# k and v of the last two pairs through two levels of seven products, their chain on VectorE

## The chip, the cores and the metric

One core of one Trainium2 chip runs the whole program. The metric is the device time of one execution in microseconds (us). Engine names in the profile: PE is TensorE's matrix multiplies, PEld its weight loads, DVE is VectorE, ACT is ScalarE, POOL is GpSimd, SP issues the DMAs. All data is float32.

## The reference

The input `x` is 8 sequences of 512 tokens by 512 features. After a layernorm `xn`:

```python
q = xn @ Wq.T + bq;  k = xn @ Wk.T + bk;  v = xn @ Wv.T + bv
phi_q, phi_k = elu(q) + 1, elu(k) + 1
kv_sum = cumsum(phi_k * v, axis=1)                  # along the tokens
s = (phi_q * kv_sum) * 32 ** -0.5 @ Wo.T + bo
g = silu(ffn(xn))    # Hadamard transforms folded into weights; gate and up 512 -> 2048, down 2048 -> 512
out = x + s * g
```

## The kernel before, in words

**Pairs.** The sequences are worked on two at a time, so the loop over `p` has four pairs of 1024 tokens. For each pair: attention projections k, v, q; four hidden units of the feed-forward part (gate and up for 512 hidden features each); `project_out`; and `down` in two halves, after units 1 and 3. Features lie on the 128 partitions, tokens along the free dimension.

**Seven products in place of eight.** Every matrix product is cut into 2 x 2 blocks and done with seven block products (P1 to P7) and sums of blocks. The factors of the weights are made once and kept in DRAM; the factors of the tokens, `xo`, are made per pair by `inner_tokens` and `inner_t3`.

- One level: `group` (products on line 460) does k, v, q with 128x512 products. One call covers two of the four feature blocks of k, v or q, seven products of two matmuls each; k and v need four calls a pair.
- Two levels: `block_product` (products on line 638) does one of the seven outer products by seven inner ones, each two matmuls of 128x256. `hidden_unit` calls it seven times, in the order P1, P5, P6, P2, P7, P3, P4, with gate and up as the two lanes. This is how all hidden units but three of pair 0 are done.

**Reading PSUM.** In a `block_product` each of the seven inner products is followed by a read: `px` (three banks) is read after its products 1, 3, 4 and 5 of the chain into `sa`, `sb`, `sc` or straight to the output; `py` (one bank) and `pz` (two banks) are added to those. Where the outer product adds to an earlier result (`add` is given: P6, P2, P7, P3, P4), all seven reads are on DVE; else four are copies on ACT and three are on DVE (lines 646 to 680). A bank is free for the next product only after its read.

**Attention before.** `with_k` makes elu(k)+1 from two ACT activations and one DVE instruction per half (lines 710 to 712); `with_v` multiplies (724); `sums` runs the cumulative sum (729); `with_q` makes the context `co` (737), whose token factors POOL makes (`encode_tokens`, lines 304 to 307).

**Units.** In `hidden_unit` POOL adds tiles (lines 838 and 842), ACT applies Silu (828), POOL or, in units 1 and 3, DVE multiplies gate by up (829) and makes the token factors of `ho` (823).

**Order.** An agenda (`at`, `advance`) places the steps of a group by hand, so that the products of two neighbours interleave. `later` puts small steps into a list that `pace` takes from after an output has been issued; `catch_up` empties it. A scheduler then orders the instructions of each engine; every engine works through its own list in order. `queue` is the order in which weights are streamed in, three ahead, through four buffers; loads and stores are issued by SP in order. Working tiles of 8 KB a partition come from the pool `t8`, which has six buffers: a new tile waits until an old one has been read for the last time.

Of the kernel before, what the change touches and what calls it, by code (L numbers as in the profile page):

```python
# [21 lines left out]
def kernel(  # L22
# [81 lines left out]
    at = 0  # L104
# [12 lines left out]
    had = const.tile([P, P], F32, tag="had", name="had")  # L117
    ones = const.tile([P, 1], F32, tag="ones", name="ones")
    su_ug = const.tile([P, KD], F32, tag="su_ug", name="su_ug")
    su_dp = const.tile([P, NF], F32, tag="su_dp", name="su_dp")  # L120


# [207 lines left out]
    def stream_w(name):  # L330
        w = new_w("%s_%s" % (name[0], name[1] if type(name[1]) is int else "%d_%d" % name[1]))
        if name[0] == "gu":
            u, i = name[1]
            nc.sync.dma_start(w, inner[u][:, i])
        elif name[0] == "down":
            h, i = name[1]
            assert wd_made[h] == 4
            w = by_factor(w, 4)
            nc.sync.dma_start(w, wd[h][:, i])
        else:  # L340
            nc.sync.dma_start(flat(w), kept["%s_%d" % name])
            if name[0] == "o":
                w = by_factor(w)
        return w
# [77 lines left out]
        later(0.0, at, 8, last, soon=True)  # L422

    agenda = []
# [199 lines left out]
        between()  # L627


    def block_product(name, w, x, out, add, done):  # L630


        px, py, pz = (bank(t, name, 2) for t in ("px", "py", "pz"))
        sums = {}

        def product(p, i, first):
            for lane in range(2):
                nc.tensor.matmul(  # L638
                    p[:, lane], w[:, lane, i, :], x[:, i, :],
                    start=(first and lane == 0), stop=True, skip_group_check=True,  # L640
                )

        def read(what, m, q):
            s = snap.tile([P, 2, H], F32, tag="s", name=f"{what}_{name}")
            if add is None:
                nc.scalar.copy(s, px)
            else:
                nc.vector.tensor_tensor(s, px, add[:, m, :, q], ALU.add)  # L648
            return s

        def p1():
            product(px, P1, True)
            sums["a"] = read("sa", 0, 0)

        def p2():
            product(py, P2, True)
            nc.vector.tensor_tensor(out[:, 0, :, 0], sums["a"], py, ALU.add)

        def p7():
            product(pz, P7, True)  # L660

        def p6():
            product(px, P6, False)
            sums["b"] = read("sb", 1, 0)

        def p5():
            product(px, P5, False)
            sums["c"] = read("sc", 1, 1)
            nc.vector.tensor_tensor(out[:, 1, :, 1], sums["c"], pz, ALU.add)

        def p3():
            product(px, P3, False)
            if add is None:
                nc.scalar.copy(out[:, 0, :, 1], px)
            else:
                nc.vector.tensor_tensor(out[:, 0, :, 1], px, add[:, 0, :, 1], ALU.add)  # L676

        def p4():
            product(pz, P4, False)
            nc.vector.tensor_tensor(out[:, 1, :, 0], sums["b"], pz, ALU.add)  # L680
            if done:
                done()

        for place, fn in ((0, p1), (2, p2), (3, p7), (4, p6), (8, p5), (12, p3), (13, p4)):
            at(place, fn)
        advance(7)
# [2 lines left out]
    def x_rhs(xo):  # L689
        return lambda k, i: xo[:, i, k : k + 3 : 2, :]  # L690

    def attention(p, xo, co, get_w):
        def project(m, g, then):
            w = get_w(m, g)
            r = t8.tile([P, 2, 2, L], F32, tag="t", name=f"{m}_{p}_{g}")
            b = (col("b" + m, g), col("b" + m, g + 2))

            def whole(px):
                nc.scalar.activation(r[:, 0, 1], px, AF.Identity, bias=b[0])
                then(r)  # L700

            group(
                f"{m}_{p}_{g}", [w[:, 0], w[:, 1]], x_rhs(xo),
                (r[:, 0, 0], r[:, 1, 0], r[:, 1, 1]), whole, b, 1.7,
            )

        def elu_plus_one(r, name):
            neg = t8.tile([P, 2, 2, L], F32, tag="t", name=f"neg_{name}")
            for h in range(2):
                nc.scalar.activation(neg[:, h], r[:, h], AF.Relu, scale=-1.0)  # L710
                nc.scalar.activation(neg[:, h], neg[:, h], AF.Exp, scale=-1.0)
                nc.vector.scalar_tensor_tensor(r[:, h], r[:, h], 1.0, neg[:, h], ALU.add, ALU.max)

        def heads(g):
            phi = {}
# [23 lines left out]
                    )  # L739
                encode_tokens(nc.gpsimd, co[:, g])  # L740

            project("k", g, with_k)
            project("v", g, with_v)
            project("q", g, with_q)

        for g in range(2):
            heads(g)


    def put_by(name, t):  # L750
# [56 lines left out]
            (r[:, 0, 0], r[:, 1, 0], r[:, 1, 1]), with_up,  # L807
        )

    def hidden_unit(p, u, xo, ho, get_w, last):  # L810

        def new(name):
            return t8.tile([P, 2, 2, 2, H], F32, tag="t", name=f"{name}_{p}_{u}")

        def outer(i, out, add=None, done=None):
            w = get_w("gu", (u, i))
            block_product(f"gu_{p}_{u}_{i}", w, xo[:, i], out, add, done)

        def whole(t, lane):
            return t[:, :, lane].rearrange("p m q t -> p m (q t)")  # L820

        def sub(eng, c, a, b):
            eng.tensor_tensor(ho[:, :, c], ho[:, :, a], ho[:, :, b], ALU.subtract)

        def gated(t, a, s, eng):
            g = whole(t, 0)
            for m in range(2):
                nc.scalar.activation(g[:, m], g[:, m], AF.Silu, scale=col("w_gate", u + m * NU + a * NG))  # L828
            eng.tensor_tensor(ho[:, :, (P1, P7, P2, P3)[2 * a + s]], g, whole(t, 1), ALU.mult)

        eng = nc.vector if last else nc.gpsimd
        ra, rv, ru1 = new("a"), new("v"), new("u1")
        rest = {}

        def with_u1():
            rest["u3"] = r = new("u3")
            for m in range(2):
                nc.gpsimd.tensor_tensor(r[:, m], ru1[:, m], rv[:, m], ALU.add)  # L838

        def with_r():  # L840
            for m in range(2):
                nc.gpsimd.tensor_tensor(rv[:, m], rv[:, m], rr[:, m], ALU.add)  # L842
            gated(rv, 1, 1, nc.gpsimd)

        def with_c12():
            gated(rest["u3"], 0, 1, eng)
            sub(eng, P5, P7, P1)
            sub(eng, P6, P3, P5)
            sub(eng, P7, P3, P7)

        def with_c21():
            gated(ru1, 1, 0, eng)
            sub(eng, P4, P2, P6)

        outer(P1, ra)
        outer(P5, rv)
        outer(P6, ru1, ra, with_u1)
        outer(P2, ra, ra, lambda: gated(ra, 0, 0, nc.gpsimd))
        rr = new("r")
        outer(P7, rr, ru1, with_r)  # L860
        while "u3" not in rest:
            advance(1)
        outer(P3, rest["u3"], rest["u3"], with_c12)
        outer(P4, ru1, rr, with_c21)

    def down(p, half, hos, get_w, ds=None, ss=None, ys=None):
        if half == 0:
# [212 lines left out]

    queue = []
    for p in range(B // 2):
        queue += [(p, m, g) for g in range(2) for m in ("k", "v", "q")]
        for u in range(NU):
            if p == 0 and u < NU - 1:
                queue += [(p, m, f) for m in ("gate", "up") for f in (u, u + NU)]
            else:
                queue += [(p, "gu", (u, i)) for i in (P1, P5, P6, P2, P7, P3, P4)]
            if u == 0:
                at_o = len(queue) - (2 if p == 0 else 0)  # L1090
                queue[at_o:at_o] = [(p, "o", 0), (p, "o", 1)]
            if u % 2:
                queue += [(p, "down", (u // 2, i)) for i in (P1, P7, P2, P6, P5, P3, P4)]
# [56 lines left out]
    for b in range(2):  # L1150
        transposed(b, xs[b], xo)
    nc.vector.memset(ones, 1.0)
    nc.vector.tensor_scalar(su_ug, col("su_ug", 0, KD), D ** -0.5, None, ALU.mult)
    nc.vector.scalar_tensor_tensor(
        su_dp, col("su_dp", 0, NF), FF ** -0.5, col("w_up", 0, NF), ALU.mult, ALU.mult
    )
# [45 lines left out]
    for p in range(B // 2):  # L1202
        if p:
            catch_up()
            inner_tokens(xo)
            co = hop.tile([P, 2, 7, L], F32, tag="h", name=f"co_{p}")
        attention(p, xo, co, get_w)
        if p:
            catch_up()
            inner_t3(xo, (P1, P5, P6, P2, P7))  # L1210
            at(9, lambda: inner_t3(xo, (P3, P4)))
        more = p + 1 < B // 2
        hos = []
        for u in range(NU):
# [8 lines left out]
            else:  # L1223
# [4 lines left out]
                    with background():  # L1228
                        normalized(3)
                ho = hop.tile([P, 2, 7, L], F32, tag="h", name=f"ho_{p}_{u}")  # L1230
                hidden_unit(p, u, xo, ho, get_w, u % 2 == 1)
                if u == 0:
                    project_out(p, co, get_w)
            hos.append(ho)
            if more and u < 2 and (p, u) != (0, 1):
# [2 lines left out]
            if u == 1:  # L1238
                if p == 0:
                    weights_ahead(NU - 1)  # L1240
                    inner_tokens(xo, 6)
                down(p, 0, hos, get_w)
                hos = []
        ds = [fetch(f"d_{p}_{s}") for s in range(2)]
# [59 lines left out]
```

## Time and profile before

| what | value |
| --- | --- |
| median of 3 runs | 1551.32 us (1550.75 to 1551.83) |
| span of the profiled execution | 1552.4 us |
| granted TensorE clock, mean | 0.998 |
| PE busy | 1523.8 us, 98% |
| DVE busy | 1002.4 us, 65% |
| ACT busy | 418.9 us, 27% |
| POOL busy | 436.7 us, 28% |
| one pair (first k product of pair 1 to that of pair 2, by the chain of waits) | 460.67 to 823.82 us |

The page gives no time for the profiled execution other than its span, which lies 1.1 us above the median of the runs; times worked out on the trace are set against the span, and 1.1 us is taken off to compare with runs. A line of the timeline has the start in us, the time from the first start to the last end in us, the engine, the line, the operation, tiles, shapes and the number of records merged. TensorE leaves two records for each float32 matmul in the program. An instruction's own time has an end that overlaps with the next; the spacing of starts in an unbroken stream is what one more instruction costs.

### The profile page before, as it was taken

How to read it: one execution, taken by the hardware profiler on the slowest of the kernel's cores; microseconds unless marked ns; L12 is line 12 of the kernel's file. 1: busy time of each engine (PE TensorE's matmuls, PEld its weight loads, DVE VectorE, ACT ScalarE, POOL GpSimd, SP SyncE). 2: the span in 40 equal slices, each digit the busy share in tenths (PEclk: the TensorE clock that was granted, in tenths of full speed). 3: DMA queues.
4: the chain of work that ended last, by engine and by line, in shares of the span. 5: the costliest groups of instructions: out<-in, count | busy, mean ns of one | idle time of the engine just before them, and what ended most of it. 6: DMA issues, size and time to landing. Idle time of an engine off the chain costs nothing.

```text
span 1552.4 us, 15693 instructions
## 1 busy us (share of the span) xinstructions
PE 1523.8 (98%) x5924; PEld 1121.3 (72%) x5924; DVE 1002.4 (65%) x1423; ACT 418.9 (27%) x664; POOL 436.7 (28%) x236
## 2 busy tenths in 40 slices
PE   7989999999999999999999999999999999999998
PEld 3436446746874588888884488888886478888887
DVE  7989787378867665516767674715675575533673
ACT  4452341141125411112114431111213431111211
POOL 1232233004320261205511144302621126210631
PEclk9999999999999999999999999999999999999999
DMA  8345877687985244354576344335574233535462
GB/s 276 98 141 176 258 250 240 214 276 261 267 283 162 90 154 160 95 166 164 166 265 235 93 143 149 114 119 186 175 245 155 87 112 102 191 100 174 164 258 81
DMA packets 197692, 273.31 MB, mean 176 GB/s; under 512 B 56816, under 2 KB 155120, under 8 KB 193392
## 3 DMA queue, kind: packets, MB, share of 16 engines
q1 hardware_dynamic: 197472, 272.27, 54.0%
q8 instruction: 47, 0.77, 0.2%
q14 instruction: 29, 0.24, 0.0%
q10 hardware_dynamic: 144, 0.03, 0.0%
HBM read 196.25 MB, written 76.02 MB: 175 GB/s over the span
## 4 chain that ended last, share of the span: by engine, by line
PE 90%; DVE 6%; DMA 1%; ACT 1%; issue 1%; SPq 0%; POOL 0%; POOLq 0%; DVEq 0%; ACTq 0%
PE px_gu L638 20%; PE px_dn L536 13%; PE pz_gu L638 10%; PE pz_dn L536 6%; PE py_gu L638 5%; PE px_k L460 4%; PE py_dn L536 4%; PE px_o L536 3%; PE px_v L460 3%; PE px_q L460 3%; PE px_up L460 2%; PE pz_o L536 2%; PE pz_k L460 2%; PE pz_v L460 2%; PE pz_q L460 2%; PE px_gate L460 1%
## 5 line engine op out<-in xcount | busy, mean ns | idle before, releaser
L638 PE MATMUL px_gu<-xo,w_gu 128*128 128x256 f32 x1456 | 347.7, 380 | 1.4 <-DVE sb_gu L648 1.4
L638 PEld LDWEIGHTS px_gu<-xo,w_gu 128*128 128x128 f32 x1456 | 275.7, 190 | 45.9 <-issue 5.0
L536 PE MATMUL px_dn<-w_down,ho 128*128 128x256 f32 x1024 | 228.7, 379 | 0.0
L536 PEld LDWEIGHTS px_dn<-w_down,ho 128*128 128x128 f32 x1024 | 194.6, 190 | 28.6 <-issue 2.4
L638 PE MATMUL pz_gu<-xo,w_gu 128*128 128x256 f32 x728 | 187.7, 380 | 1.1 <-DVE u L476 1.1
L838 POOL TENSOR_TENSOR u<-u,v 128x1024 f32<-128x1024 f32 x26 | 61.0, 2367 | 365.9 <-DVE u L676 347.4
L638 PEld LDWEIGHTS pz_gu<-xo,w_gu 128*128 128x128 f32 x728 | 137.5, 190 | 22.3 <-DVE u L476 1.5
L536 PE MATMUL pz_dn<-w_down,ho 128*128 128x256 f32 x496 | 112.5, 379 | 1.7 <-DVE u L476 1.7
L536 PEld LDWEIGHTS pz_dn<-w_down,ho 128*128 128x128 f32 x496 | 93.7, 190 | 16.4 <-DVE u L476 2.1
L638 PE MATMUL py_gu<-xo,w_gu 128*128 128x256 f32 x364 | 93.4, 379 | 0.0
L304 POOL TENSOR_TENSOR co<-co 128x512 f32<-128x512 f32 x8 | 14.6, 1829 | 266.3 <-DVE co L737 266.3
L883 POOL TENSOR_TENSOR s<-s,d 128x512 f32<-128x512 f32 x30 | 40.0, 1333 | 165.4 <-ACT d L882 165.4
L638 PEld LDWEIGHTS py_gu<-xo,w_gu 128*128 128x128 f32 x364 | 69.2, 190 | 9.4
L842 POOL TENSOR_TENSOR v<-v,r 128x1024 f32<-128x1024 f32 x26 | 60.9, 2361 | 26.9 <-DVE r L676 26.9
L460 PE MATMUL px_k<-xo,w_k 128*128 128x512 f32 x128 | 61.8, 606 | 0.0
L460 PE MATMUL px_v<-xo,w_v 128*128 128x512 f32 x128 | 60.6, 594 | 0.0
L460 PE MATMUL px_q<-xo,w_q 128*128 128x512 f32 x128 | 60.3, 592 | 0.0
L828 ACT ACTIVATE a<-a,cols_sb 128x512 f32<-128x512 f32 x26 | 18.7, 721 | 149.5 <-DVE a L676 147.8
L882 ACT ACTIVATE d<-d 128x512 f32<-128x512 f32 x31 | 19.5, 630 | 144.4 <-DVE d L551 124.7
L536 PE MATMUL px_o<-w_o,co 128*128 128x256 f32 x256 | 58.2, 379 | 0.0
L828 ACT ACTIVATE u<-u,cols_sb 128x512 f32<-128x512 f32 x52 | 36.9, 720 | 78.2 <-DVE u L676 75.0
L536 PE MATMUL py_dn<-w_down,ho 128*128 128x256 f32 x256 | 57.9, 379 | 0.0
(269 smaller groups left out, 2417.4 us busy)
## 6 DMA issues: line engine op xcount, KB each, us to landing
w_gu<-d_gu SPq DMA_DIRECT2D x91, 896.0 KB, 4.5
w_down<-d_down SPq DMA_DIRECT2D x56, 512.0 KB, 3.8
d_s<-o SPq DMA_DIRECT2D x8, 1024.0 KB, 5.7
d_d<-dn SPq DMA_DIRECT2D x8, 1024.0 KB, 7.7
d<-d_d SPq DMA_DIRECT2D x8, 1024.0 KB, 6.3
s<-d_s SPq DMA_DIRECT2D x8, 1024.0 KB, 8.1
y<-in_x_dram SPq DMA_DIRECT2D x8, 1024.0 KB, 6.4
out_dram<-y SPq DMA_DIRECT2D x15, 512.0 KB, 3.2
```

What stands on the lines that cost most here:

```text
L304: eng.tensor_tensor(o[..., P5, :], o[..., P7, :], o[..., P1, :], ALU.subtract)
L460: nc.tensor.matmul(p.rearrange("p a t -> p (a t)") if len(r.shape) == 2 else p, ws[k][:, i, :], r, start=(first and k == 0), stop=(k == n ...
L536: nc.tensor.matmul(p[:, c], t[:, (2 * g + c) * P : (2 * g + c + 1) * P], ws[i](k), start=(first and k == 0 and c == cs[0]), stop=(k == n - ...
L638: nc.tensor.matmul(p[:, lane], w[:, lane, i, :], x[:, i, :], start=(first and lane == 0), stop=True, skip_group_check=True,)
L828: nc.scalar.activation(g[:, m], g[:, m], AF.Silu, scale=col("w_gate", u + m * NU + a * NG))
L838: nc.gpsimd.tensor_tensor(r[:, m], ru1[:, m], rv[:, m], ALU.add)
L842: nc.gpsimd.tensor_tensor(rv[:, m], rv[:, m], rr[:, m], ALU.add)
L882: nc.scalar.activation(d, d, AF.Silu)
L883: (nc.vector if final and (a, s) == (1, 0) else nc.gpsimd).tensor_tensor(r, r, d, ALU.mult)
```

## The change

For pairs 2 and 3, k and v are no longer done by `group` but by the two-level scheme, with k and v as the two lanes of `by_blocks`, which is `hidden_unit`'s sequence of seven `block_product`s cut out into a function of its own. q stays with `group`, and comes first.

- The weight factors of the second level are made during `down(1, 0)`, four calls of `factors_kv` (k and v, outer products 0 to 3 and 4 to 6): each loads kept factors, stores three as they are and four after one DVE sum each, with SP issuing loads and stores.
- In `attention_by_blocks` the whole of one quarter of k and v is known when its last outer product has been read. Then ACT makes the Relu and Exp, and a chain of DVE steps is put into the idle list: elu(k)+1 with the bias (`positive`, two of 128x512), times v with its bias (`weighted`, two), the cumulative sum (`scan`, two, with a vector of ones that lies in PSUM), and the context (`context`, one of 128x1024). There are four chains a pair. POOL makes the token factors of `co` by four subtractions of 128x1024.
- The chains are paced out over the outputs of kv and of the hidden unit that follows; `finish` empties the list before `project_out`.
- `positive`'s scratch is in the places of `co` that are made last. The tiles `v` and `u1` of `by_blocks` are asked for after the first outer product.
- Weights: seven loads of `kv` in place of four of k and v a pair.

```diff
-    def block_product(name, w, x, out, add, done):
+    def block_product(name, w, x, out, add, done, time=0):
...
+        def output(o, s, p):
+            pace(nc.vector.tensor_tensor(o, s, p, ALU.add), time if add is None else time / 2)
...
+    def attention_by_blocks(p, xo, co, get_w):
+        one = ps.tile([P, 1], F32, tag="t", name=f"one_{p}")
...
+        def heads(t, a, s):
+            k, v = (t[:, :, lane].rearrange("p m q t -> p m (q t)") for lane in range(2))
+            place = (P1, P7, P2, P3)[2 * a + s]
+            neg = co[:, :, (P4, P6, P4, P5)[2 * a + s]]
...
+            nc.scalar.activation(neg, neg, AF.Exp, scale=-1.0)
+            def positive(m):
+                nc.vector.scalar_tensor_tensor(
+                    k[:, m], k[:, m], bk1[:, m + 2 * a : m + 2 * a + 1], neg[:, m], ALU.add, ALU.max
+                )
+            def weighted(m):
+                nc.vector.scalar_tensor_tensor(
+                    v[:, m], v[:, m], col("bv", m + 2 * a), k[:, m], ALU.add, ALU.mult
+                )
+            def scan(m):
+                nc.vector.tensor_tensor_scan(
+                    k[:, m], one.to_broadcast([P, L]), v[:, m], 0.0, ALU.mult, ALU.add
+                )
+            def context():
+                c = co[:, :, place]
+                nc.vector.scalar_tensor_tensor(c, k, QSCALE, c, ALU.mult, ALU.mult)
+                made.append(place)
+                if place == P7:
+                    sub(P5, P7, P1)
+                    sub(P6, P3, P5)
+                    sub(P7, P3, P7)
+                if place == P2:
+                    sub(P4, P2, P6)
+            def chain():
+                for us, step in ((0.6, positive), (0.6, weighted), (1.2, scan)):
+                    for m in range(2):
+                        later(us, step, m)
+                later(1.2, context)
+            at(9 if a and s else 4, chain)
+        by_blocks(p, "kv", xo, lambda i: get_w("kv", i), heads, 1.1)
...
+        if p < 2:
+            queue += [(p, m, g) for g in range(2) for m in ("k", "v", "q")]
+        else:
+            queue += [(p, "q", g) for g in range(2)]
+            queue += [(p, "kv", i) for i in (P1, P5, P6, P2, P7, P3, P4)]
...
-                hidden_unit(p, u, xo, ho, get_w, u % 2 == 1)
+                hidden_unit(p, u, xo, ho, get_w, u % 2 == 1, 1.1 if p > 1 and u == 0 else 0)
                 if u == 0:
+                    heads_made()
                     project_out(p, co, get_w)
...
+                if p == 1:
+                    for i, (m, lo, hi) in enumerate((("k", 0, 4), ("k", 4, 7), ("v", 0, 4), ("v", 4, 7))):
+                        at(2 + 12 * i, lambda m=m, lo=lo, hi=hi: factors_kv(m, lo, hi))
```

## The prediction

> **What bounds the kernel now.** I read the page's first part, then the list of who waited for whom, then the sums by stretch for pair 2.
>
> ```profile
> PE 1523.8 (98%) x5924; PEld 1121.3 (72%) x5924; DVE 1002.4 (65%) x1423; ACT 418.9 (27%) x664; POOL 436.7 (28%) x236
> ```
> ```profile
> PE px_gu L638 <- DVE sb_gu L648: 1.4, 1, 1.4
> PE pz_gu L638 <- DVE u L476: 1.1, 1, 1.1
> ```
> ```profile
> 889.25:932.65 43.40, 43.40 (x193) 36.23 (x192) 33.47 (x48) 13.94 (x19) 18.00 (x10) 1.00 0.40 132
> 636.00:690.00 54.00, 54.00 (x252) 47.46 (x251) 15.44 (x19) 8.04 (x13) 2.26 (x1) 1.00 0.41 124
> 823.66:889.25 65.59, 65.59 (x154) 28.78 (x153) 44.38 (x57) 30.44 (x37) 5.67 (x5) 1.00 0.49 148
> ```
>
> TensorE sets the time: it is busy 98%, and over the whole run the largest wait of a hidden unit's product for DVE is 1.4 us. The columns of the stretches are length, then busy time of PE, PEld, DVE, ACT, POOL, the clock, the DMA share and GB/s. The first is hidden unit 0 of pair 2, the second `down` of pair 1, the third the attention of pair 2. PE has no idle time in any. But DVE is already busy 33.5 of 43.4 us in the unit and 44.4 of 65.6 in the attention, so what is put on it there has little room.
>
> **What TensorE saves.** Starts of products in an unbroken stream:
>
> ```profile
> 884.10 1.88 PE L460 MATMUL pz_v<-xo,w_v 128*128 128x512 f32 x4
> 885.82 1.88 PE L460 MATMUL pz_q<-xo,w_q 128*128 128x512 f32 x4
> ...
> 908.48 1.89 PE L638 MATMUL px_gu<-xo,w_gu 128*128 128x256 f32 x8
> 910.21 1.03 PE L638 MATMUL py_gu<-xo,w_gu 128*128 128x256 f32 x4
> ```
>
> Four records are two matmuls of the program. Of 512 columns, two take 885.82 - 884.10 = 1.717 us (the digits from more such rows), 0.858 each. Of 256 columns, four take 1.727 us, 0.432 each. k and v took 4 calls x 7 products x 2 = 56 matmuls x 0.858 = 48.1 us a pair; they now take 7 x 7 x 2 = 98 x 0.432 = 42.3 us. That is 5.8 us a pair, **11.5 us in all**. q is unchanged and only moved ahead. The weights come as in a hidden unit, 896 KB for every 6.0 us of products, and there no product waits for a load.
>
> **What it puts on DVE.** Unit costs are start to start:
>
> ```profile
> 884.78 2.33 DVE L729 TENSOR_TENSOR_SCAN k<-ones,v 128x512 f32<-128x512 f32 x2
> 887.03 0.67 DVE L476 TENSOR_TENSOR v<-sb_v,pz_v 128x512 f32<-128x512 f32 x1
> ...
> 899.54 1.22 DVE L737 SCALAR_TENSOR_TENSOR co<-k,q 128x1024 f32<-128x1024 f32 x1
> 900.67 1.22 DVE L712 SCALAR_TENSOR_TENSOR q<-q,neg_q 128x1024 f32<-128x1024 f32 x1
> ...
> 910.41 0.69 DVE L648 TENSOR_TENSOR sc_gu<-px_gu,a 128x512 f32<-128x512 f32 x1 [0.17 <-PE px_gu L638]
> 911.13 0.69 DVE L669 TENSOR_TENSOR u<-sc_gu,pz_gu 128x512 f32<-128x512 f32 x1
> 911.74 0.68 DVE L657 TENSOR_TENSOR a<-sa_gu,py_gu 128x512 f32<-128x512 f32 x1
> ```
>
> A 128x512 instruction costs 0.61 us (911.13 to 911.74), 0.11 more if it needs the one just before (910.41 to 911.13); a scan 1.13 (2.25 for two); a 128x1024 product 1.13. A chain of the change is two `positive`, two `weighted`, two scans and a context: 4 x 0.61 + 2 x 1.13 + 1.13 = 5.8 us, four chains 23.3 us a pair. Before, k and v had 30 us of DVE work over 65.6 us. Now the reads of kv alone are 2 x 3 + 5 x 7 = 41 instructions, 25 us in 42.3, and the chains can begin only when a quarter of k and v is whole: after the fourth of seven outer products, plus Relu and Exp. All four must end before `project_out`.
>
> So I count the stretch from the first chain to the end of hidden unit 0, in the order in which the changed program's instructions stand. DVE has 82 there: 54 reads of PSUM and 16 half products (70 x 0.61 = 42.7), 8 scans (9.1), 4 contexts (4.6), nine that need the one before (1.0): **57.4 us**. TensorE has 65 pairs of matmuls of 256 columns, 65 x 0.863 = **56.1 us**. With no wait at all DVE has become the longer queue.
>
> **POOL beside it.** Four rows show DVE and POOL together:
>
> ```profile
> 201.43 4.51 DVE L93 TENSOR_TENSOR rd<-rd 128x1024 f32<-128x1024 f32 x2
> 1134.10 1.42 DVE L829 TENSOR_TENSOR ho<-u 128x1024 f32<-128x1024 f32 x1 [0.79 <-ACT u L828]
> ```
> ```profile
> 202.00 2.85 POOL L802 TENSOR_TENSOR ho<-g,u 128x1024 f32<-128x1024 f32 x1 [4.45 <-DVE u L476]
> 1132.07 2.36 POOL L829 TENSOR_TENSOR ho<-v 128x1024 f32<-128x1024 f32 x1 [0.83 <-ACT v L828]
> ```
>
> Two DVE products with both operands in SBUF, 2.4 us otherwise, took 4.51 when POOL's 2.85 us instruction began between them: the second waited to POOL's end. At 1134.10 the wait is 0.2, to 1134.43. Reads of PSUM beside POOL keep 0.68. A hidden unit by `block_product` with POOL's help has so far had only PSUM reads on DVE; `positive`, `weighted` and `context` are products of two SBUF operands, put among POOL's adds of 2.36 us. By the order I find five that start inside a POOL instruction: the second `positive` of the first chain (behind `v` + `r`, 2.1 us), one `positive` and two `weighted` of the last chain (behind the three subtractions on `co`, 1.9, 1.8, 1.1), the last context (behind the unit's own `v` + `r`, 1.9). Together 8.8 us; the bounds are 0, if each falls in a gap, and 12, one full 2.36 for each of five.
>
> The scan's ones now lie in PSUM; no scan in this trace has such an operand. It lies between 1.13 (as a read of PSUM beside POOL) and 1.13 + 2.36; I take 1.13, since the nearest row is that of a read with one operand in PSUM; at the other end four scans beside POOL add up to 4 x 2.36 = 9.4 us a pair. The Trainium skill (GPSIMD Engine Reference, Key points) says that POOL contends with DVE instructions that have two SBUF inputs or run in a 2-port mode. By that page the sum keeps its 8.8 and nothing is added for the scans.
>
> **Idle time within DVE's queue.** The tile `r` of hidden unit 0 finds `t8` full and waits for the slot of `a`, whose last reader is POOL after two Silu: 1.0 us of DVE idle. ACT's copies of the first products of the unit stand behind the Relu of the last two chains, which wait for the last reads of kv: 1.9 us. One more wait for a product is 0.6. Sum 3.4.
>
> **Sum.** 57.4 + 8.8 + 3.4 = 69.6 us of DVE against 56.1 us of products: TensorE, which can run ahead only by three `px` banks and one `py`, must wait **13.5 us a pair**. Two pairs: +27.0 - 11.5 = +15.5, and 1552.4 + 15.5 = 1567.9 as a span, 1566.8 as a run (1.1 less, as before).
>
> **The factors, and what else is moved.** Sixteen DVE sums of 128x512 or less in `down` of pair 1 are at most 9.8 us, where DVE is busy 15.4 of 54 us and reads of PSUM come in every 1.7 us or more: nothing. Without that cover they would cost the 9.8. The eight loads and 28 stores stand in SP's queue between the weights of `down`, the stores behind DVE's sums. A weight lasts 6.9 us there and is loaded three ahead, and the page has no product waiting for a DMA; I take 0, bounds 0 and 5 (one load landing a factor's load and store late). POOL loses 16 small factors of `co` in two pairs and gets eight subtractions; ACT keeps its work. Neither is a bound, but ACT's order costs the 1.9 above.
>
> **Rivals.**
>
> - *The chains are covered, faster.* DVE's chains slip between POOL's work, and PSUM's banks smooth the rest: about 1 us of waits a pair, as a pair of before has (823.82 - 460.67 = 363.15 us, against products of 84 x 0.858 for k, v and q, 4 x 42.3 for the units, 56 x 0.432 for `project_out` and 224 x 0.432 for `down`, 362.2). Then -11.5 + 2 = -9.5: 1541.8. For it: the steps are paced out over the outputs of two units. Against it: 57.4 against 56.1 before any wait. It decides if the reads of PSUM keep within one product of their places.
> - *No contention, but the rest.* 57.4 + 3.4 - 56.1 = 4.7 a pair against 5.8: -2.2 in all, 1549.1.
> - *More on DVE.* Scans wait too, up to the 9.4, or stores hold up a weight: with 8 us a pair more, 1566.8 + 16 = 1583.
> - *The saving isn't there*, because 256-column products are held by weight loads (190 ns of each 216). Against it: the unit's products already run at 0.432 with them. It would add 11.5 and is held within the last case.
>
> **How the numbers follow.** The sum's case 0.62 (its own range 1557 to 1576, five waits of 0.9 to 2.36 and idle of 1 to 5), covered 0.16, no contention 0.12, more 0.10. The likeliest gives 1566.8. The range runs from 1547, which takes in the third of these and leaves out the covered case, to 1580, half of the last: 0.21 is left out. This measurement tells 0.2%, 3.1 us, from no change. Faster by more: the covered case and a little of the next, 0.18. Within: 0.10. Slower: 0.72.
>
> **What would show it.** After: k and v as 128x256 products at 0.432; PE waits for DVE, a total near 27 us, in hidden unit 0 of pairs 2 and 3 and nowhere else; DVE without idle there; `positive`, `weighted` and the context with means above 0.69 and 1.22, scans at 1.22; pair 1's `down` as long as before. The prediction is wrong if PE's waits for DVE stay under 6 us a pair, or if DVE's products keep their length beside POOL.

## The result and the profile after

The changed kernel takes **1572.36 us** (median of 4 runs, 1571.28 to 1574.4) against 1551.03 us before (4 runs): 1.0134 times as long, 95% interval 1.0121 to 1.0148. That is 21.3 us slower, inside the range and 5.6 us above the forecast. Its profiled execution has a span of 1569.5 us, 17.1 more than before.

First the page's busy line and rows of the list of who waited for whom, of the changed kernel (us in total, times, longest).

```profile
PE 1527.1 (97%) x6092; PEld 1156.0 (74%) x6092; DVE 1054.0 (67%) x1517; ACT 409.5 (26%) x656; POOL 460.0 (29%) x236
```
```profile
...
PE py_gu L677 <- DVE u_gu L691: 3.7, 2, 1.8
PE pz_dn L575 <- DVE u L515: 3.5, 1, 3.5
PE px_o L575 <- DVE r_gu L718: 3.3, 2, 1.6
PE pz_up L499 <- DVE u L515: 3.0, 1, 3.0
PE px_gu L677 <- DVE sb_gu L687: 2.8, 5, 0.9
...
```

Two kinds of wait stand out. Those on `py_gu`, `px_o` and, but for one of 0.8 us in pair 0, `px_gu` occur in hidden unit 0 and `project_out` of pairs 2 and 3; the unit was foretold, `project_out` was not. Those on `pz_dn` and `pz_up` lie in pair 0, where the change was not expected to do anything. Before, the same two were 1.7 and 0.8 us.

Now the sums by stretch for pair 2: kv, hidden unit 0, and `project_out` with the start of unit 1.

```profile
849.77:893.51 43.74, 43.64 (x194) 36.16 (x193) 33.69 (x52) 16.85 (x24) 9.80 (x4) 1.00 0.60 174
893.51:938.85 45.34, 41.10 (x182) 33.09 (x180) 43.69 (x59) 12.31 (x18) 13.26 (x6) 1.00 0.47 148
938.85:972.36 33.51, 32.80 (x141) 27.46 (x142) 22.27 (x29) 4.23 (x6) 26.28 (x11) 0.95 0.22 79
```

In hidden unit 0 DVE is busy 43.7 of 45.3 us (33.5 of 43.4 before), and TensorE stands idle for 4.2. The third row shows a clock of 0.95: just after the wait the granted clock was half for 3.4 us. The products of kv run at the pace that was worked out, eight records in 1.73 us:

```profile
884.44 1.89 PE L677 MATMUL px_kv<-xo,w_kv 128*128 128x256 f32 x8
886.17 1.03 PE L677 MATMUL pz_kv<-xo,w_kv 128*128 128x256 f32 x4
```

The two queues at the end of hidden unit 0 show why DVE is late. POOL first, then DVE:

```profile
932.54 7.86 POOL L814 TENSOR_TENSOR co<-co 128x1024 f32<-128x1024 f32 x3 [1.94 <-DVE co L843]
940.36 5.13 POOL L949 TENSOR_TENSOR v_gu<-v_gu,r_gu 128x1024 f32<-128x1024 f32 x2
946.32 2.37 POOL L975 TENSOR_TENSOR ho<-v_gu 128x1024 f32<-128x1024 f32 x1 [0.83 <-ACT v_gu L973]
```
```profile
932.97 2.46 DVE L827 SCALAR_TENSOR_TENSOR u_kv<-u_kv,bk,co 128x512 f32<-128x512 f32 x1
935.36 0.68 DVE L691 TENSOR_TENSOR u_gu<-sa_gu,py_gu 128x512 f32<-128x512 f32 x1
935.95 2.23 DVE L832 SCALAR_TENSOR_TENSOR u_kv<-u_kv,cols_sb 128x512 f32<-128x512 f32 x1
...
939.31 1.64 DVE L832 SCALAR_TENSOR_TENSOR u_kv<-u_kv,cols_sb 128x512 f32<-128x512 f32 x1
...
943.26 2.33 DVE L837 TENSOR_TENSOR_SCAN u_kv<-one,u_kv 128x512 f32<-128x512 f32 x2
...
947.28 2.49 DVE L843 SCALAR_TENSOR_TENSOR co<-u_kv,co 128x1024 f32<-128x1024 f32 x1
```

`positive` and `weighted` take 0.74 us where POOL is still; beside its three subtractions they take 2.46, 2.23 and 1.64. A PSUM read at 935.36 keeps 0.68, and the two scans at 943.26, beside POOL's sums on `v_gu`, keep 1.17 each. The first chain's first `positive` (2.25 at 887.84) and the last context (2.49, 1.22 elsewhere) make five long products a pair.

Where the time went is seen best from the first product of each pair, by the timeline; before the change, that of pair 1 starts at 457.07 us, and the chain of waits, which gave 460.67, enters the pair 3.6 us later. Each row is one profiled execution. The table gives the time from the start of the span to pair 1, the lengths of pairs 1 and 2, and of pair 3 up to its last `down`, with the experiments that follow.

| kernel | to pair 1 | pair 1 | pair 2 | pair 3 | median of runs |
| --- | --- | --- | --- | --- | --- |
| before | 457.1 | 363.2 | 363.1 | 311.9 | 1551.0 |
| changed | 465.9 | 363.1 | 367.1 | 315.9 | 1572.4 |
| factors_alone | 467.3 | 363.1 | 363.1 | 311.9 | 1564.7 |
| no_chain | 471.1 | 363.1 | 357.0 | 305.9 | 1554.8 |
| pool_cut | 469.3 | 364.5 | 361.0 | 309.9 | 1563.2 |
| on_pool | 468.0 | 363.4 | 374.3 | 321.0 | 1583.3 |
| consts_last | 455.4 | 363.2 | 367.1 | 315.9 | 1561.1 |
| before_shifted | 467.5 | 363.2 | 363.2 | 311.9 | 1566.7 |
| ones_in_sbuf | 456.3 | 363.5 | 375.5 | 322.8 | 1579.9 |
| late_context | 458.0 | 363.2 | 371.0 | 320.5 | 1571.8 |
| early_chain | 460.3 | 363.1 | 367.0 | 315.9 | 1565.0 |
| out_later | 459.7 | 363.1 | 367.1 | 315.9 | 1563.3 |
| spread | 458.2 | 363.2 | 368.7 | 317.6 | 1565.7 |
| spread_co_first | 455.9 | 363.8 | 366.1 | 314.9 | 1560.4 |

Pairs 2 and 3 lose 4.0 us each. Another 8.8 us are lost in pair 0, where every engine has the same instructions in the same order, but for four small ones on DVE: two on 128x4 that make the constants `nbk` and `bk1`, and two that set the scans' ones (128x1). So there are two causes to find. The kernel before was timed again beside each group of experiments, with medians of 1551.0 to 1555.7; ratios below are to the one beside the run.

### The profile page after: what moved, and what is told of

Its sections match the earlier page's. It is cut to its first block, busy times and chain, and to the rows that moved or that the text cites. A ratio compares the mean times of both kernels' runs of the same rounds, so it can differ in the third digit from the quotient of the medians.

```text
span 1569.5 us, 16210 instructions
## 1 busy us (share of the span) xinstructions
PE 1527.1 (97%) x6092; PEld 1156.0 (74%) x6092; DVE 1054.0 (67%) x1517; ACT 409.5 (26%) x656; POOL 460.0 (29%) x236
## 5 line engine op out<-in xcount | busy, mean ns | idle before, releaser
L945 POOL TENSOR_TENSOR u_gu<-u_gu,v_gu 128x1024 f32<-128x1024 f32 x26 | 61.0, 2369 | 402.3 <-DVE u_gu L718 389.6
L949 POOL TENSOR_TENSOR v_gu<-v_gu,r_gu 128x1024 f32<-128x1024 f32 x26 | 61.8, 2399 | 22.5 <-DVE r_gu L718 22.5
L921 POOL TENSOR_TENSOR ho<-g,u 128x512 f32<-128x512 f32 x6 | 12.5, 2079 | 159.2 <-DVE u L515 152.1
L973 ACT ACTIVATE a_gu<-a_gu,cols_sb 128x512 f32<-128x512 f32 x26 | 18.5, 722 | 153.1 <-DVE a_gu L718 151.8
L575 PEld LDWEIGHTS px_o<-w_o,co 128*128 128x128 f32 x256 | 49.0, 192 | 12.0 <-DVE r_gu L718 4.1
L967 POOL TENSOR_TENSOR ho<-ho 128x1024 f32<-128x1024 f32 x24 | 56.3, 2357 | 1.3
L973 ACT ACTIVATE u_gu<-u_gu,cols_sb 128x512 f32<-128x512 f32 x52 | 36.8, 722 | 75.8 <-DVE u_gu L718 72.3
```

The source lines that it names most:

```text
L575: nc.tensor.matmul(p[:, c], t[:, (2 * g + c) * P : (2 * g + c + 1) * P], ws[i](k), start=(first and k == 0 and c == cs[0]), stop=(k == n - ...
L921: nc.gpsimd.tensor_tensor(ho[:, P1], g[:, 0, 0], r[:, 0, 0], ALU.mult)
```

## The experiments

**factors_alone: no kv, but its factors and constants.**

```diff
-        heads_made = (attention if p < 2 else attention_by_blocks)(p, xo, co, get_w)
+        heads_made = attention(p, xo, co, get_w)
```

> Attention as before in all four pairs; the two constants, the factors of k and v in the second pair's down and by_blocks as after. The factors are made but nothing reads them. Theory (the factors are free, and the 8.8 us that the first pair lost are TensorE clock dips which the attention of pairs 2 and 3 has nothing to do with): pairs 1, 2 and 3 as long as before, 363.1 us each; the first pair either 457 (if its dips are chance of one execution: time 1551) or about 466 (if they come with the small shift at the start: 1560). Rival (factors, loads and stores cost something): pair 1 longer than 363.2 by up to 9.8.

Measured 1564.7 us, 1.0063 (1.0048 to 1.0078). Pairs 1 to 3 are as before to 0.1 us, and pair 1's `down` half takes 50.94 us as before (50.93), though DMA there is busy 0.78 in place of 0.40. The factors are free. But the first pair has lost 10.3 us, without any work on kv, and in all four runs of it (1564.4 to 1565.1).

**no_chain: the steps of the chain left out.** `positive`, `weighted`, `scan` and `context` are not made; reads, activations and POOL's work stay.

> positive, weighted, scan and context are left out, with all else as after, so co holds q and not the context, and the output is not the reference's. Theory (TensorE saves 5.8 us a pair, and the chain on DVE costs 9.7): pairs 2 and 3 take 363.1 - 5.8 = 357.3 each, 1572.4 - 2 x 9.7 = 1553 with the first pair's 8.8 us, 1544 without. Rival (products of 256 columns are held by weight loads, so that the saving is not there): pairs 2 and 3 at 363 or more, 1564 or more.

Measured 1554.8 us, 1.0004 (0.9994 to 1.0013). Pair 2 takes 357.0 and pair 3 305.9: 6.1 and 6.0 us less than before. The saving on TensorE is there, and the chain alone takes it away and 4.0 more.

**pool_cut: POOL's adds beside the chain made short.**

```diff
-            nc.gpsimd.tensor_tensor(co[:, :, c], co[:, :, a], co[:, :, b], ALU.subtract)
+            nc.gpsimd.tensor_tensor(co[:, :, c, :32], co[:, :, a, :32], co[:, :, b, :32], ALU.subtract)
```

> In pairs 2 and 3 POOL's subtractions on co work on 32 of 512 columns, and its v + r of kv and of hidden unit 0 on 8 of 128; order, waits and every product are as after, so the output is not the reference's. Theory (DVE's products of two SBUF operands wait to the end of POOL's instruction): the five long ones of a pair fall from 1.6 to 2.5 us back to 0.7 and 1.2, DVE has 7.1 us a pair less, TensorE's loss falls from 9.7 to about 3 a pair: 1572.4 - 14 = 1558. Rival (DVE's queue is too long by itself, 57.4 us of instructions against 56.1, or its idle time decides): 1568 or more.

Measured 1563.2 us, 1.0050 (1.0032 to 1.0068). The edit cuts `v` + `r` of kv and of hidden unit 0 too, to 8 of 128 columns. The total is 5 us above what was expected; the first pair (469.3) and pair 1 (364.5) are longer by 3.4 and 1.4. In the pairs that the edit touches the expectation holds: 361.0 and 309.9, 6.1 and 6.0 us less than the changed kernel. The long products are gone, by the sums by line:

```profile
L827 DVE SCALAR_TENSOR_TENSOR u_kv<-u_kv,bk,co 128x512 f32<-128x512 f32 x8 | 6.0, 765 | 0.0
L832 DVE SCALAR_TENSOR_TENSOR u_kv<-u_kv,cols_sb 128x512 f32<-128x512 f32 x8 | 5.8, 742 | 0.0
...
L843 DVE SCALAR_TENSOR_TENSOR co<-u_kv,co 128x1024 f32<-128x1024 f32 x4 | 4.9, 1216 | 0.0
```

The means (the last number but one) were 1178, 1346 and 1850 ns in the changed kernel. Between pool_cut and no_chain lie 4.0 us a pair: the price of the chain without POOL beside it.

**on_pool: the chain's products on POOL, its biases on ACT.** ACT makes relu(k + bias) and the scaled v, POOL adds, multiplies and makes the context.

> The products of the chain leave DVE: ACT makes relu(k + bias) and the scaled v with its bias, POOL adds, multiplies and makes the context, DVE keeps the scans. The result is the same function. Theory (only DVE's queue and its waits for POOL cost): DVE has 20 instructions fewer in the stretch and no product of two SBUF operands, 43 us against 56.1 of TensorE, so pairs 2 and 3 come to 358 to 360 each, 1553 to 1557 with the first pair's 8.8 us, 1544 to 1548 without. Rival (POOL, with 19 to 29 us more, is late with its adds, or the context is late for project_out): 5 us or more lost in each pair, 1563 or more.

Measured 1583.3 us, 1.0177 (1.0150 to 1.0204). The theory falls; the rival holds, with 11 and 9 us lost in the pairs. By the list of waits:

```profile
PE px_gu L678 <- ACT sa_gu L686: 11.7, 2, 5.9
...
PE px_gu L678 <- DVE sa_gu L688: 6.6, 2, 3.3
```

ACT's fourteen activations for two chains stand ahead of its copies for hidden unit 0, and DVE's read into `sa_gu` waits 5.3 us for POOL's sum of `u_gu`, which stands behind the contexts and subtractions on `co`. A free engine is no cover where its queue is in the way of another product.

**consts_last and before_shifted: where the tiles lie in SBUF.** `nbk` and `bk1` take 32 bytes of a partition each. They are allocated ahead of all working tiles, so that `xo`, the weights and the tiles of `t8` start 64 bytes later in the built program: `xo` at byte 20,032 of a partition in place of 19,968, which is 78 x 256. One kernel puts the constants behind all other tiles; the other gives the kernel before an unused tile of 64 bytes.

```diff
-    nbk = const.tile([P, KD], F32, tag="nbk", name="nbk")
+    nbk = small.tile([P, KD], F32, tag="nbk", name="nbk", bufs=1)
```
```diff
+    blank = const.tile([P, 16], F32, tag="blank", name="blank")
```

> The changed kernel with its two new constants, nbk and bk1 (32 bytes of a partition each), allocated behind all other tiles in place of ahead of them, so that every working tile has the SBUF address that it has in the kernel before; instructions and their order are the same. Theory (the 64 bytes move every working tile off its multiple of 256, DMA of such tiles is slower, and the first pair, where DMA is busy 72%, pays for it): the first pair back from 466 to about 457, stores of s_gate from 4.0 back to 3.4 us, the pairs after it as in the changed kernel: 1572.4 - 9 = 1563. Rivals (the two extra DVE instructions at the start, the place of d_kv in DRAM, or chance): the first pair stays at 465 or more, 1570 or more.

> The kernel before with an unused tile of 64 bytes a partition among its constants; not one instruction is added. Theory (SBUF addresses): the first pair 466 to 470 in place of 457, stores of s_gate 4.0 us in place of 3.4, time 1551 to 1554 + 9 to 13 = 1560 to 1566. Rival (something else of the change slows the first pair): as before, 1551 to 1554.

Both theories hold, the second with a time 0.7 us above its range. consts_last took 1561.1 us, 1.0044 (1.0028 to 1.0060), with 455.4 us to pair 1. before_shifted, in which no instruction was added, took 1566.7, 1.0079 (1.0063 to 1.0095), with 467.5. The transfers of the first 457 us, of before and then of before_shifted (KB each, median us from issue to landing):

```profile
d_gu<-s_gate SPq DMA_DIRECT2D x16, 448.0 KB, 3.4
...
d_down<-wd SPq DMA_DIRECT2D x4, 896.0 KB, 4.7
```
```profile
d_gu<-s_gate SPq DMA_DIRECT2D x16, 448.0 KB, 4.0
...
d_down<-wd SPq DMA_DIRECT2D x4, 896.0 KB, 5.9
```

The same stores take 18 and 26% longer from issue to landing, and loads beside them land later too, those of `w_gu` after 6.9 us in place of 6.1. In one place a load ends last: DVE's wait for a part of `w_gate`, just ahead of the products `pz_dn`, of the kernel before and of the changed one:

```profile
247.74 0.94 DVE L937 TENSOR_TENSOR r_gate<-w_gate 128x512 f32<-128x512 f32 x1 [1.95 <-DMA w_gate<-in_wgate_t_dram]
```
```profile
251.36 0.98 DVE L1056 TENSOR_TENSOR r_gate<-w_gate 128x512 f32<-128x512 f32 x1 [3.14 <-DMA w_gate<-in_wgate_t_dram]
```

TensorE then waits for DVE, in before_shifted as in the changed kernel: 3.5 us on `pz_dn` in both, 2.9 and 3.0 on `pz_up`. In consts_last they are back at 1.8 and 0.8 us. All kernels with the shift reach pair 1 at 465.9 or later, all without it at 460.3 or earlier. Pair 1 has the same length in both; DMA is busy for 0.50 of it in the kernel before, against 0.71 of what precedes it.

Longer waits are the smaller part of what the changed kernel loses in pair 0. The stretch to pair 1, of before, of before_shifted and of the changed kernel:

```profile
0.00:457.07 457.07, 434.22 (x1388) 262.17 (x1389) 362.30 (x538) 152.71 (x287) 119.69 (x81) 1.00 0.71 226
```
```profile
0.00:467.47 467.47, 438.66 (x1388) 265.36 (x1389) 357.47 (x538) 153.34 (x287) 123.47 (x81) 0.98 0.72 221
```
```profile
0.00:465.88 465.88, 441.14 (x1389) 266.36 (x1390) 357.34 (x542) 153.43 (x287) 122.34 (x81) 0.98 0.72 222
```

Of the changed kernel's 8.8 us TensorE is idle for 1.9 (24.7 against 22.9); for 6.9 it is busy longer with the same products, as the granted clock was half for 20.5 us, in three dips, against 3.4 before. In before_shifted it is 6.0 of idle time and 4.4 of busy time, with 17.1 us at half clock. Two of the changed kernel's dips come with the waits on `pz_dn` and `pz_up`. The third comes with a wait of 3.7 us that the kernel before has too; late_context and ones_in_sbuf, without the shift, have a dip as long there, so the runs do not put that one down to the shift.

The remaining kernels have the constants as in consts_last, and 1561.1 us is what they are to be held against; the kernel before took 1553.2 to 1555.7 beside them, 1554.2 beside consts_last.

**ones_in_sbuf: the scan's ones in SBUF.**

> The constants as in the kernel consts_last; the scans take their ones from the SBUF column that the first two pairs use, not from PSUM. Theory (two SBUF operands wait to the end of POOL's instruction, whatever the operation): scans beside POOL rise from 1.22 to 2 us and more, 2 to 9.4 us a pair, 4 to 19 us above consts_last. Rival (a broadcast column is read once and does not count as a second SBUF operand): scans stay at 1.22, within 2 us of consts_last.

Measured 1579.9 us, 1.0167 (1.0149 to 1.0185): 18.7 us more than consts_last, at the upper end. The scans of the two chains beside POOL:

```profile
L837 DVE TENSOR_TENSOR_SCAN u_kv<-ones,u_kv 128x512 f32<-128x512 f32 x8 | 22.0, 2775 | 0.0
```

They took 1.21 us with the ones in PSUM. So the scan waits for POOL as the products do once both its operands are in SBUF, even where one is a single column.

**late_context and early_chain: another order, another pace.** late_context holds the third context, which releases POOL's three subtractions, back until the fourth chain has made its products. early_chain also doubles the pace in hidden unit 0.

```diff
+                    if step is scan and place == P2:
+                        later(1.2, held.pop())
```

> The constants as in the kernel consts_last; the context of the third chain is made after positive and weighted of the fourth and not ahead of them, so that POOL's three subtractions on co, which it releases, run beside scans with their ones in PSUM and beside reads of PSUM. Theory (three of the five long products come from these subtractions): 1.8 + 1.5 + 1.0 = 4.3 us a pair less than consts_last, 1563 - 8.6 = 1554, and no positive or weighted of the fourth chain above 0.8 us. Rival (DVE's queue is too long in any order, or the tile of the third chain, held for longer, makes a new tile wait): within 2 us of consts_last.

> late_context with twice the pace in hidden unit 0 (2.2 in place of 1.1), so that the chains end some 10 us earlier and POOL's subtractions are done when project_out begins. Theory (late_context lost what it gained because the subtractions had become late, 4.4 us before pz_o): that wait goes, the fourth chain keeps 0.75 us a product, and what is left is the queue's length, 4 us a pair, and the first chain's wait: 362 a pair, 1561 - 10 = 1551. Rival (DVE's queue moves the wait to the unit's own products): waits of 4 us or more for px_gu in hidden unit 0, 1557 or more.

In late_context the fourth chain is at 0.75 us a product, as foretold, and the time is 1571.8 us, 1.0112 (1.0096 to 1.0128), 10.7 more than consts_last: the theory on the time falls. The subtractions are now what ends last:

```profile
PE pz_o L575 <- POOL co L815: 8.2, 2, 4.4
```

early_chain takes this wait away, keeps the short products, and has 1565.0 us, 1.0065 (1.0049 to 1.0080), with pairs of 367.0 and 315.9, the same as consts_last. The rival holds. The waits of pairs 2 and 3 are now spread over the unit, 8.8 us in six on `sa_gu` and 2.2 in three on `sb_gu`. The expected gain went there; that twice the pace puts more on DVE within one outer product than it has free is the likely reason, and was not tested by itself.

**out_later, spread and spread_co_first: a later deadline.** out_later puts `project_out` behind P1 and P5 of hidden unit 1.

> Constants as in consts_last; in pairs 2 and 3 project_out, and with it the point by which all four chains must end, comes after the second outer product of hidden unit 1 in place of after hidden unit 0, and the chains are paced out over the outputs up to there. Theory (in the stretch to project_out DVE has more to do than TensorE, and waits come from the deadline: two more outer products, P1 and P5, where DVE has three reads of seven, give it 12.1 us of products for about 4 us of reads): the waits of 1.8 to 2.0 us at the end of hidden unit 0 and their clock dips go, pairs 2 and 3 come from 367 to 359 to 362, consts_last 1561 - 10 to 16 = 1545 to 1551, below the kernel before. Rival (the waits are those of single products beside POOL, wherever the chain ends, or tiles held longer make others wait): 364 or more a pair, 1555 or more.

Measured 1563.3 us, 1.0062 (1.0049 to 1.0075), pairs as in consts_last to 0.1 us. The rival holds: the waits of 1.85 and 1.63 us stay where they were, though the deadline had gone. The chains kept their place all the same, the fourth context at 941 us and `project_out`'s first read at 953, since every output takes at least one step, whatever it costs. spread lets budgets add up instead:

```diff
+        credit[0] = min(credit[0] + us, 1.4)
+        while (urgent or idle) and credit[0] >= (urgent or idle)[0][0]:
```

> out_later with a slower pace: the outputs of kv and of hidden units 0 and 1 take a step only when their budgets (0.6 us an output where DVE makes seven reads of an outer product, 1.4 where it makes three) have added up to its cost, where before each output took at least one step whatever it cost; and the first chain starts 5 us later, behind POOL's v + r. The fourth chain and POOL's subtractions then fall into P1 and P5 of hidden unit 1, where DVE has 1.8 us of reads in 6.0 us of products. Theory (TensorE waits where DVE gets more than its free 1.5 us in one outer product, be it by steps or by waits for POOL; out_later changed neither): about 5 us of waits a pair less than consts_last, pairs 2 and 3 at 360 to 363, 1561 - 8 to 14 = 1547 to 1553, about the time of the kernel before or below. Rival (in any order and at any pace some 10 us a pair are lost, since tiles and banks are held for as long): 366 or more a pair, 1560 or more.

Measured 1565.7 us, 1.0069 (1.0055 to 1.0083). The rival's 366 or more a pair came true, but by another wait than it named. Of the waits in hidden unit 0 of pair 2 two are left, 1.5 and 0.4 us, but there is a new one, of 6.1 us, which makes the pair 1.6 us longer than in consts_last:

```profile
953.51 3.78 PE L585 MATMUL pz_o<-w_o,co 128*128 128x256 f32 x8 [6.14 <-POOL co L824]
```

POOL had three subtractions on `ho` of unit 0, 8.75 us, ahead of those on `co` in its queue. The last kernel turns these two about.

> spread, with POOL's four subtractions on ho of hidden unit 0 put behind the three on co in POOL's queue. In spread the waits of kv and hidden unit 0 had shrunk to one of 1.5 us, and project_out's pz waited 6.1 us for the subtractions on co, which stood behind 8.75 us of subtractions on ho; TensorE's clock then dropped for 6.8 us. Theory (that wait is nothing but POOL's order): it falls to 0 to 1 us, the dip goes, and pairs 2 and 3 come from 368.7 to 359 to 361: 1565.7 - 16 to 19 = 1547 to 1550, below the kernel before on the same chip by 4 to 8. Rival (POOL has too much in this stretch in any order): a wait of 3 us or more for POOL stays, there or for a later tile, 1555 or more.

Measured 1560.4 us, 1.0054 (1.0040 to 1.0069), pairs of 366.1 and 314.9. `pz_o` still waits, 2.3 us, now for a read on DVE that stands behind the fourth chain's products beside those subtractions, and 1.1 us follow on `pz_gu`. So neither account holds whole: the wait for POOL went, and the time did not follow it. Pairs 2 and 3 are 1.0 us shorter each than in consts_last, but by the ratios, 1.0054 and 1.0044, the two cannot be told apart. No version with kv by blocks that leaves nothing out is faster than the kernel before.

## Why the prediction was near, and where it was wrong

The span was forecast as 1567.9 and is 1569.5. That is nearer than its reasons deserve: pairs 2 and 3 were to bring +15.5 and brought +8.0, and 8.8 us came from a pair that the prediction left at nothing. Of the 5.6 us of the miss, 1.6 are in the span; the other 4.0 are the step from span to run, where 1.1 us were taken off and the changed kernel's median stands 2.9 above its profiled span. Taking them off was wrong: every run on record that has both is 1.7 to 1.9 us above its own span, so that the profiled execution before, of 1552.4, was one of about 1554.2 us (an estimate), slower than all four runs of that kernel. The spans therefore show 17.1 of the 21.3 us.

- **TensorE saves 5.8 us a pair**: right, 6.1 by no_chain. The rival of the weight loads is out.
- **DVE's queue, 57.4 against 56.1 us, and 3.4 us of idle time**: right in kind. Without POOL's contention the chain costs 4.0 us a pair, where 4.7 were added up; DVE's idle time is 1.8 us, not 3.4.
- **POOL beside it, 8.8 us a pair**: the mechanism and four of the five places are right (in the first chain it was the first `positive`, not the second), the size is not. The long products hold 1.5 + 1.7 + 1.5 + 0.9 + 1.3 = 6.9 us more than undisturbed ones, and TensorE got 6.1 back in pool_cut. The starts within POOL's instructions were set too early, and the last context stood behind a gate product, not behind `v` + `r`.
- **The sum, 13.5 us of waits a pair**: 4.0 + 5.8 = 9.8 measured, by the lengths. They do not all lie in hidden unit 0, as it said: `project_out` has its part, and in pair 2 a clock dip follows. The prediction called itself wrong if PE's waits for DVE stayed under 6 us a pair, and by the list of waits they did: 4.6 us in pair 2 and 5.8 in pair 3, far from 27 in all. The list shows only part of the loss. Pair 2 is 10.1 us longer than in no_chain, and TensorE stands idle for 5.0 of them; a record of 128x256 lasts 0.38 us and the next starts 0.216 after it, so that a start up to 0.16 us late leaves no idle time, and the dip adds up to 1.7. The sign was set on a measure that misses such delays, which the prediction did not see.
- **Scans at 1.13**: right (1.22 as an instruction's own time), and for the reason given. The rule of the Trainium skill (GPSIMD Engine Reference, Key points), by which POOL contends with DVE instructions of two SBUF inputs, is borne out by these runs: 1.21 us beside POOL with one SBUF operand, 2.78 with two.
- **The factors at 0**: right.
- **The failed step** is the one on what else is moved. It counted instructions, loads and stores, put the rest at nothing, and did not see that two constants move every tile allocated after them. before_shifted prices that at 12.5 us on its chip, consts_last at 11.2 between the medians. One term of 9 to 12 us was missing, what was added up for pairs 2 and 3 was 7.5 too large, and they nearly cancelled: the near hit was luck.

The Trainium skill has a rule that bears on the missing term (DMA: Bandwidth & Descriptors, How a descriptor splits into AXI transactions): a transaction has to begin at a multiple of 256 bytes, so that a descriptor that starts elsewhere needs more beats. By that page a piece of 512 bytes that starts 64 bytes past a multiple takes 18 beats in place of 16, an estimate of 12% more. The stores above took 18 and 26% more, but with time in queues in it, and the single packets do not bear the estimate out: by the traces, packets of 512 bytes took 27.3 ns on the mean before and 28.3 in before_shifted, 27 at the median in both. Packets of 128 bytes, the loads of `z`, went from 13.0 to 18.8. Only shifts by 64 bytes, and by 96 in on_pool with its third constant, were tried, so that the runs show the cost of the shift, and neither that 256 is the boundary nor how the shift slows the transfers.

What stays open: a version with aligned tiles, the whole computation and no contention was not found. pool_cut says what is to be had, 6 us a pair, which with aligned tiles would be about 1561 - 12 = 1549, some 5 below the kernel before beside it (1554.2); this is an estimate and was not run. Every order tried gave back most of it, or more, to a wait on POOL or on a read.

## What to carry to other kernels

Before a new constant is put ahead of the working tiles, see what it does to their addresses: an unused 64 bytes cost more here than the change itself. Where a stretch is as full as this one (DVE busy 43.7 of 45.3 us), count what an engine has free within one product and its buffers, and give a step to it only when that has added up: in spread this took most waits out of the unit, though a new one, on POOL, cost as much again. Moving the deadline or the order alone turned one wait into another here. Price a DVE product of two SBUF operands beside POOL to the end of POOL's instruction, as it was here, and take an operand that can lie in PSUM from there.

## What the runs showed of the hardware

The same wait in pair 0 costs more in one execution than in another. TensorE waits 3.7 us there for ACT (`pwd`) in both kernels, with the same work after it. The stretch around it, of the changed kernel and of the one before:

```profile
105.60:112.40 6.80, 5.49 (x7) 2.39 (x8) 3.55 (x7) 6.77 (x12) 0.00 (x0) 0.50 0.96 287
```
```profile
105.30:112.10 6.80, 5.50 (x13) 2.58 (x14) 3.56 (x7) 6.77 (x12) 0.00 (x0) 1.00 1.01 313
```

TensorE is busy for as long, but at a granted clock of 0.50 it gets 7 records done in place of 13. Over all fourteen profiled executions the dips, but for one at the end of each span, last 3.4 or 6.8 us and come with waits of some 1.6 to 6 us, not with every one of them. So a wait may cost up to 3.4 us more than its length (6.8 us at half clock), and not in every execution: one more reason why the time to pair 1 scatters by some 5 us within each group of the table.
